# An attention block on one core: GpSimd takes the normalisations, the softmax sums are kept apart, and the last tiles go out singly

## The chip, the cores and the metric

The kernel runs on one core of a Trainium2 chip. A core has five engines with a queue of instructions each: TensorE (PE, matmuls and transposes), VectorE (DVE), ScalarE (ACT, activation functions by table), GpSimd (POOL) and SyncE (SP, here only a queue for transfers). Each works through its queue in order and waits on semaphores for what other engines produce. PE writes its results into PSUM, which this kernel uses as eight banks of 128 x 512 fp32; ACT and DVE read these here, POOL does not. The metric is the device time of one execution in microseconds.

## What is computed

Eight sequences of 512 tokens with 256 channels, all in fp32, run through one transformer block:

```
x = x + attn(layernorm(x))
x = x + ffn(layernorm(x))      # routed: 4 of 16 blocks of hidden units
x = x + gla(layernorm(x))      # gated linear attention over batches, then a SwiGLU
x = x + ffn(layernorm(x))
```

The change lies in the attention and in the very last store. The attention has 16 heads of 16 channels, and only 307 of the 512 queries of a head keep their result:

```
scores   = q @ k.T / 4
sparsity = scores.max(-1) - scores.mean(-1)
top      = top_k(sparsity, 307)
out      = 0 outside top;  softmax(scores[top]) @ v inside
y        = out @ Wo + bo
layernorm(x) = (x - mean(x)) / sqrt(var(x) + 1e-5)
```

## The kernel before

The block holds all tokens in one SBUF tile, `xres` (128 partitions x 8 batches x 4 token tiles x 256 channels). Instructions are written in program order, tile by tile; a planner then sets the order on each engine by simulating the queues with its own estimates of durations, earlier program order first where several instructions could start. So an instruction can be queued well ahead of where the program has it if its inputs are there. To hold an instruction back, the kernel writes one element of its output with a POOL copy from a tile that is made late (`late` in the code); the true write then has to follow that copy.

**The attention's pipeline.** The work is cut into 128 steps, numbered n: batch, head group m (2), parity e (2) and query tile k (4). For each step `max_one` makes four score tiles of 128 x 512 (contraction over 32 rows, one of four row strips each), and DVE reduces each to its maxima (L490). Sixteen steps later (`LAG`) `exp_one` makes the same scores transposed, ACT takes the exponential (L502), and `weigh` multiplies by the values (L507). `take` moves the sum of a head group to SBUF: the weighted values into `outC`, the softmax denominators by a small transfer on ACT's queue into rows of `den`, one row per batch and head. The maxima go through PE (`place_maxima`, L450) into `neg` and into spare rows of q.

**The fronts.** `front(b)` makes q, k and v of one batch: xn (the normalised tokens), its transposes (L357), the copy `xnT` and a copy `xcT` with the mean over tokens taken off, and then the projections q, k (L384) and v (L423) with their evictions (L397, L402, L414, L432). It is a generator, taken in pieces between the groups of scores. In steps 0 to 13 (`LEAD`) there are no exponentials yet, and the pieces of the fronts 0 and 1 are spread over them (`alone` is true); from step 14 on front b+2 runs while batch b has its exponentials.

**The statistics.** `batch_stats` gives mean and variance by `bn_stats` and `bn_aggr` on DVE (L275, L276), the root on ACT (L279), then on DVE the reciprocal (L280) and the shift -mean/root (L283). Batch 0's run at the start, batch 1's in step 1, batch 2's in step 5, batch 3's from step 16, those of 4 to 7 together from step 29. The norms themselves run in `front`: on DVE (L344), for batch 1 on ACT (L340). Loads of x for batch 2 onwards hang on maxima (L217). ACT holds one table of functions at a time; Sqrt and Exp are in different ones, and a change costs an `ACT_TABLE_LOAD`.

**The end of attention.** After the last maxima `top_queries` marks the chosen queries (26 rounds on DVE). `weights_of` makes from `den` the factor of each query and row (reciprocal L137, product L138), for six batches together and later for batches 6 and 7. `weigh_outputs` spreads the rows over channels with a matmul on a strip of 32 rows (L150; two batches share a strip, batch 0 with 1 and so on), and DVE multiplies `outC` by it (L153). `out_unit` projects two batches for one token slice (L163), with the eviction on ACT and the addition on POOL; the other slices are projected later (L849).

**The store.** In the last routed layer each pair of batches of a token slice is added in one DVE instruction (L969) and stored in one transfer (L972).

## Time and profile before

Four runs took 1624.45 to 1631.8 us, median 1628.25. The profile is of one execution.

| | us |
|---|---|
| the profiled execution | 1630.65 |
| its span, first to last instruction | 1628.7 |
| PE busy | 1591.7 (98%) |
| DVE busy | 971.6 (60%) |
| ACT busy | 676.5 (42%) |
| POOL busy | 348.8 (21%) |
| first group of scores starts | 16.1 |
| first exponential starts | 69.9 |
| last `outC` of attention by DVE starts after | 603.84 |
| last addition by DVE starts | 1624.97 |

PE's busy time is modelled and includes waits inside a group of matmuls, so a busy PE need not be PE at its peak; the granted clock is in a row of its own. In a list of groups each line has the source line, engine, operation, output and inputs with shapes, the count, the busy time in us with the mean ns of one, and the idle time ahead of it with the instruction that ended it. In a list by time each line has start, duration, engine, source line and operation; `[1.40 <-ACT e L502]` says that the engine was idle for 1.40 us until that instruction ended.

### The profile page before, as it was taken

What the parts mean: (1) busy time and instruction counts of PE and PEld (TensorE: products, weight loads), DVE (VectorE), ACT (ScalarE), POOL (GpSimd) and SP (SyncE); (2) the same over time, 40 slices, a digit from 0 to 9 for tenths busy, and PEclk for the clock granted to TensorE, in tenths of its full rate; (3) what the DMA queues carried; (4) which work ended last, traced back from release to release, by engine and by line L of the source; (5) the groups of instructions that cost most, each with busy time, mean ns of one, the idle gap of its engine ahead of it and who ended that gap; (6) DMA issues with size and microseconds to landing.
All of it is one profiled execution on the core that took longest, in us unless ns stands there. A gap on an engine that the chain in (4) does not pass through costs nothing.

```text
span 1628.7 us, 19814 instructions
## 1 busy us (share of the span) xinstructions
PE 1591.7 (98%) x7444; PEld 814.3 (50%) x7444; DVE 971.6 (60%) x2007; ACT 676.5 (42%) x1215; POOL 348.8 (21%) x403
## 2 busy tenths in 40 slices
PE   7999999999999999999989999999999999999999
PEld 3323233233233256665564566545655655766666
DVE  6877777676777885447753566367265633344342
ACT  2365666556565844352346124522621452121010
POOL 2111111110010033125432343145234320000000
PEclk8999999999999999999999999999999999999999
DMA  3100000000000033000000001000000010011100
GB/s 107 43 3 3 2 2 3 2 3 3 2 3 3 3 91 105 19 22 13 1 0 1 1 0 27 1 0 1 1 0 1 1 27 0 21 33 39 40 27 26
DMA packets 24951, 27.62 MB, mean 17 GB/s; under 512 B 6872, under 2 KB 21400, under 8 KB 24856
## 3 DMA queue, kind: packets, MB, share of 16 engines
q1 hardware_dynamic: 24040, 25.31, 5.4%
q8 instruction: 58, 0.95, 0.2%
q10 hardware_dynamic: 816, 1.05, 0.2%
q14 instruction: 37, 0.30, 0.1%
HBM read 21.24 MB, written 4.33 MB: 16 GB/s over the span
## 4 chain that ended last, share of the span: by engine, by line
PE 78%; DVE 11%; ACT 4%; POOL 3%; issue 2%; DMA 1%; SPq 0%; ACTq 0%; POOLq 0%; DVEq 0%
PE y_ps L964 16%; PE h_ps L984 11%; PE s L487 9%; PE s L498 8%; PE av L507 8%; PE swi_ps L1011 7%; PE proj_ps L1097 7%; DVE pr L1130 2%; DVE pr L1120 2%; PE q_ps L384 2%; PE k_ps L384 2%; PE gla_y L1222 2%; PE v_ps L423 2%; PE chT_ps L821 2%; POOL o L1147 2%
## 5 line engine op out<-in xcount | busy, mean ns | idle before, releaser
L490 DVE TENSOR_REDUCE mx<-s 128x1 f32<-128x512 f32 x512 | 328.1, 683 | 120.5 <-PE s L498 63.5
L502 ACT ACTIVATE e<-s 128x512 f32<-128x512 f32 x512 | 276.4, 597 | 184.8 <-PE s L498 106.5
L487 PE MATMUL s<-k,q 32*128 32x512 f32 x1024 | 303.5, 649 | 3.0 <-ACT k L414 2.4
L498 PE MATMUL s<-q,k 32*128 32x512 f32 x1024 | 297.3, 642 | 0.1
L984 PE MATMUL h_ps<-xnT,w 128*128 128x512 f32 x512 | 230.1, 598 | 4.1 <-ACT h L992 4.1
L964 PE MATMUL y_ps<-w,h 128*128 128x256 f32 x1024 | 230.8, 381 | 2.7 <-DVE h L993 2.7
L964 PEld LDWEIGHTS y_ps<-w,h 128*128 128x128 f32 x1024 | 192.8, 191 | 39.3 <-issue 10.1
L984 PEld LDWEIGHTS h_ps<-xnT,w 128*128 128x128 f32 x512 | 95.2, 191 | 112.8 <-issue 106.3
L507 PE MATMUL av<-e,va 128*32 128x512 f32 (+1 forms) x1240 | 144.9, 532 | 4.6 <-ACT e L502 3.2
L993 DVE TENSOR_TENSOR h<-h,mk 128x512 f32<-128x512 f32 x128 | 98.5, 783 | 78.9 <-ACT h L992 61.2
L487 PEld LDWEIGHTS s<-k,q 32*128 32x128 f32 x1024 | 94.3, 185 | 96.2 <-DVE mx L490 52.4
L992 ACT ACTIVATE h<-h_ps,b 128x512 f32<-128x512 f32 x96 | 65.4, 685 | 174.9 <-PE h_ps L984 174.9
L969 DVE TENSOR_TENSOR xres<-xres,y_ps 128x512 f32<-128x512 f32 x48 | 32.8, 684 | 160.7 <-PE y_ps L964 123.5
L498 PEld LDWEIGHTS s<-q,k 32*128 32x128 f32 x1024 | 90.8, 183 | 75.6 <-ACT e L502 50.7
L1011 PE MATMUL swi_ps<-zT,w_gate 128*128 128x512 f32 x256 | 122.6, 599 | 4.7 <-DVE h L1020 4.6
L1011 PE MATMUL swi_ps<-zT,w_up 128*128 128x512 f32 x256 | 121.4, 594 | 0.0
L964 PE MATMUL y_ps<-w_down,h 128*128 128x256 f32 x512 | 116.9, 380 | 0.0
L1097 PE MATMUL proj_ps<-q_w,rT 128*128 128x512 f32 x256 | 116.1, 594 | 0.3 <-ACT al L1080 0.3
L964 PEld LDWEIGHTS y_ps<-w_down,h 128*128 128x128 f32 x512 | 95.7, 190 | 19.5 <-issue 8.0
L1017 ACT ACTIVATE h<-swi_ps 128x512 f32<-128x512 f32 x64 | 38.2, 596 | 155.4 <-PE swi_ps L1011 155.3
L1147 POOL TENSOR_TENSOR o<-o,pr 128x512 f32<-128x512 f32 (+2 forms) x56 | 81.1, 1449 | 58.6 <-DVE pr L1130 56.6
L507 PEld LDWEIGHTS av<-e,va 128*32 128x32 f32 x1240 | 25.5, 108 | 123.6 <-issue 103.1
(203 smaller groups left out, 1723.6 us busy)
## 6 DMA issues: line engine op xcount, KB each, us to landing
mk<-md SPq DMA_DIRECT2D x32, 256.0 KB
out<-xres SPq DMA_DIRECT2D x16, 256.0 KB
xres<-in_L_attn_a_x SPq DMA_DIRECT2D x7, 512.0 KB
q<-negT SPq DMA_DIRECT2D x128, 2.0 KB
neg<-negT SPq DMA_DIRECT2D x128, 2.0 KB
w<-in_f_w1T SPq DMA_DIRECT2D x1, 1024.0 KB
w<-in_f_w2T SPq DMA_DIRECT2D x1, 1024.0 KB
w_gate<-in_b_w_gateT SPq DMA_DIRECT2D x1, 1024.0 KB
```

Source lines behind the costliest of these rows:

```text
L487: nc.tensor.matmul(s, qs[e][rows, m, bass.ts(k, P)], ks[e][rows, m, :], start=True, stop=True)
L490: nc.vector.tensor_reduce(mx[:, b, m, e, r : r + 1], s, AX.X, ALU.max)
L498: nc.tensor.matmul(s, ks[e][rows, m, bass.ts(kt, P)], qs[e][rows, m, :], start=True, stop=True)
L502: nc.scalar.activation(ex, s, AF.Exp, scale=1.0 / DH**0.5)
L507: nc.tensor.matmul(av[32 * j : 32 * j + 32, queries], va[:, 8 * kt + 4 * m + j, e, :], es[j][:, queries], start=(kt == 0), stop=(kt == 3 a ...
L964: nc.tensor.matmul(y[0][:, bass.ts(i, D)], h[f][:, bass.ts(2 * u + i, P)], w[:, f, :], start=(f == 0), stop=(f == NF - 1),)
L984: nc.tensor.matmul(ps, w1[:, c, bass.ts(f, P)], xT[g][:, c, :], start=(c == 0), stop=(c == NC2 - 1),)
L992: nc.scalar.activation(hf, ps, AF.Relu, bias=b1[:, f : f + 1])
L993: nc.vector.tensor_tensor(hf, hf, mk[g][:, f, :], ALU.mult)
L1011: nc.tensor.matmul(ps, w[:, c, bass.ts(f, P)], zT[g][:, c, :], start=(c == 0), stop=(c == NC2 - 1),)
L1097: nc.tensor.matmul(ps, rT[b // G4][:, c, bass.ts(b % G4, P)], q_w[:, c, m], start=(c == 0), stop=(c == NC2 - 1),)
L1147: nc.gpsimd.tensor_tensor(dst, dst, src, ALU.add)
```

## The change

- Batches 1 and 2: means and variances come from ACT (`sum_stats`: four Identity and four Square activations with accumulated sums, batch 1's in step 1, batch 2's one per step from step 2). Batches 3 to 7 keep `bn_stats` on DVE, now without pauses, one tile a step from step 16.
- Roots of batches 1 to 7: on POOL, by a first guess from the bits of the number and three Newton rounds (`one_by_root`, 14 small operations), not by ACT's Sqrt. Batch 0 keeps Sqrt, followed by an Exp of one column.
- Norms: `norm` on POOL, four instructions a batch, for all batches but 0; for batches 3 to 7 at i = 12 of the 16 steps before their front, with the bias of Wo right after. The bias row is loaded in step 5 and added to batches 0 to 2 in step 11.
- Evictions in the lead: the values of fronts 0 and 1 are copied by ACT and get their bias on POOL; one more q of front 0 goes to ACT; `xcT` of batch 2 goes to ACT.
- `den` becomes two tiles, one for batches 0 to 5 and one for 6 and 7, both set to 1.0 at the start. A batch's rows move to strip b mod 4, so that the two batches of a pair lie on different strips. `weigh_outputs` does one pair at a time, and the projections of batches 0 and 1 come before the weighing of 4 and 5. The second `weights_of` covers rows 64 to 127.
- `mx` has slots for four batches, used in turn.
- In the last group of the last layer each batch is added and stored by itself.

```diff
-        def weights_of(batches, late, late_form):
-            rows = slice(16 * batches[0], 16 * batches[-1] + 16)
+        def row_of(b, m, e):
+            return 32 * (b % 4) + 16 * (b // 4) + 8 * e + 4 * m
+        def weights_of(rows, i, late, late_form):
...
-            nc.vector.reciprocal(rden[rows, :], den[rows, :])
+            nc.vector.reciprocal(rden[rows, :], den[i][rows, :])
...
-        def weigh_outputs(batches):
-            picks = itertools.cycle((bank, bank_m))
-            for u in range(2):
-                for m in range(NC2):
-                    for b in batches[u::2]:
-                        strip = bass.ts(b // 2, 32)
+        def weigh_outputs(b):
+            for m in range(NC2):
+                for c in (b, b + 1):
+                    strip = bass.ts(c % 4, 32)
...
+            for i in range(2):
+                nc.gpsimd.memset(den[i], 1.0)
...
+            def one_by_root(rs, var, scale):
+                n = rs.shape[1]
+                v = a1.tile([P, n], F32, tag="ln_v", name="ln_v")
+                u = a1.tile([P, n], F32, tag="ln_u", name="ln_u")
+                nc.gpsimd.tensor_scalar(v, var, scale, LN_EPS, ALU.mult, ALU.add)
+                nc.gpsimd.tensor_scalar(
+                    rs.bitcast(I32), v.bitcast(I32), -0.5, float(0x5F3759DF), ALU.mult, ALU.add
+                )
+                for _ in range(3):
+                    nc.gpsimd.tensor_tensor(u, v, rs, ALU.mult)
+                    nc.gpsimd.tensor_tensor(u, u, rs, ALU.mult)
+                    nc.gpsimd.tensor_scalar(u, u, -0.5, 1.5, ALU.mult, ALU.add)
+                    nc.gpsimd.tensor_tensor(rs, rs, u, ALU.mult)
+
+            def sum_stats(b, late):
...
+                own = a2.tile([P, L], F32, tag="e", name="ln_x", bufs=10)[:, 0:D]
+                for i in range(4):
+                    nc.gpsimd.tensor_copy(sums[0:1, i : i + 1], late())
+                    nc.scalar.activation(
+                        own, xres[:, b, i, :], AF.Identity, accum_out=sums[:, i : i + 1]
+                    )
+                    yield
+                nc.gpsimd.tensor_scalar(less, sums, -1.0 / D, None, ALU.mult)
+                for i in range(4):
+                    nc.gpsimd.tensor_copy(squares[0:1, i : i + 1], late())
+                    nc.scalar.activation(
+                        own, xres[:, b, i, :], AF.Square, bias=less[:, i : i + 1],
+                        accum_out=squares[:, i : i + 1],
+                    )
+                    yield
+                one_by_root(rs, squares, 1.0 / D)
...
+                norm(b, ALU.add)
+                yield
+
+            def norm(b, op=ALU.subtract, eng=nc.gpsimd):
+                xn = a2.tile([P, 4, D], F32, tag="xn", name=f"xn{b}", bufs=1)
+                for k in range(4):
+                    mean, rs = ln[b, k]
+                    eng.tensor_scalar(xn[:, k, :], xres[:, b, k, :], mean, rs, op, ALU.mult)
+                normed[b] = xn
...
-                nc.scalar.activation(rs, mv[:, :, 1], AF.Sqrt, bias=eps)
-                nc.vector.reciprocal(rs, rs)
...
-                nc.vector.scalar_tensor_tensor(sh, mv[:, :, 0], -1.0, rs, ALU.mult, ALU.mult)
+                if late is not None:
+                    one_by_root(rs, mv[:, :, 1], 1.0)
+                else:
+                    nc.scalar.activation(rs, mv[:, :, 1], AF.Sqrt, bias=eps)
+                    nc.scalar.activation(root, rs[:, 0:1], AF.Exp)
+                    nc.vector.reciprocal(rs, rs)
...
-                    if alone and b > 0:
+                    if b in (1, 2):
                         nc.scalar.mul(mean, xsum[:, c : c + 1], -1.0 / L)
                         nc.scalar.activation(xcT[:, c, :], ps, AF.Identity, bias=mean)
...
-                        if alone and (b > 0 or e == 0):
+                        if alone and (b + m > 0 or e == 0):
...
+                        if alone:
+                            nc.scalar.copy(home, v)
+                            nc.gpsimd.tensor_tensor(home, home, bias, ALU.add)
+                        else:
+                            nc.vector.tensor_tensor(home, v, bias, ALU.add)
...
-                    for _ in near.get(n, ()):
-                        pass
+                    if n == 1:
+                        for _ in early[1]:
+                            pass
+                    if n > 1:
+                        next(early[2], None)
...
+                    if (n - LEAD) % 16 == 12 and batch + 3 < NB:
+                        norm(batch + 3)
+                        add_bias(batch + 3)
...
-            weigh_outputs(range(NB - 2))
-            last = outC[NB - 3][0:1, 1, 0:1]
-            weights_of(range(NB - 2, NB), last, last)
+            for b in (0, 2):
+                weigh_outputs(b)
             for k in range(2):
-                for b in range(0, NB - 2, 2):
+                out_unit(tail, k, 0)
+            weigh_outputs(4)
+            last = outC[5][0:1, 1, 0:1]
+            weights_of(slice(P // 2, P), 1, last, last)
+            for b in (2, 4):
+                for k in range(2):
                     out_unit(tail, k, b)
-            weigh_outputs(range(NB - 2, NB))
+            weigh_outputs(6)
...
-            if i == 1 and half == 1:
+            if last and k == 3 and b == NB - 2:
+                if half == 1:
+                    x = xres[:, b + i, k, :]
+                    nc.vector.tensor_tensor(x, x, y[0][:, bass.ts(i, D)], ALU.add)
+                    nc.sync.dma_start(out=out_v[:, b + i, k, :], in_=x)
+            elif i == 1 and half == 1:
```

## The prediction

> **What bounds the kernel now.** I read the page's table of forty slices first, then the busy time in chosen stretches, VectorE's groups in one of them, and the instructions in order of time where TensorE is seen to wait.

> ```profile
> PE   7999999999999999999989999999999999999999
> PEclk8999999999999999999999999999999999999999
> ```

> TensorE (PE) is busy nearly throughout; an edit on another engine pays only where PE is held or slowed. That is slice 0, parts of the attention stage (up to 583 us), and the step to the output projection. In the stretches below the columns are length, PE, PE weight loads, VectorE (DVE), ScalarE (ACT), GpSimd (POOL), granted clock, DMA share, GB/s.

> ```profile
> 18.00:20.00 2.00, 2.00 (x5) 0.80 (x6) 1.91 (x5) 1.58 (x4) 0.17 (x1) 0.50 0.19 59
> 26.00:28.00 2.00, 2.00 (x10) 0.51 (x9) 0.00 (x0) 0.00 (x0) 0.00 (x0) 0.53 0.00 0
> 28.00:72.00 44.00, 43.28 (x189) 19.20 (x185) 42.63 (x90) 14.75 (x28) 12.57 (x19) 1.00 0.21 64
> 74.00:76.00 2.00, 2.00 (x6) 0.50 (x9) 0.42 (x1) 0.36 (x1) 0.00 (x0) 0.50 0.00 0
> ```

> From 18 to 28 us PE runs at half clock and DVE waits for it. From 28 to 72 the clock is full and DVE is occupied for 42.6 of 44 us while ACT and POOL are two thirds idle. At 72 the clock halves again, for 7 us. DVE's groups in 28 to 72:

> ```profile
> L490 DVE TENSOR_REDUCE mx<-s 128x1 f32<-128x512 f32 x57 | 35.6, 676 | 3.0 <-PE s L487 2.9
> L432 DVE TENSOR_TENSOR va<-v_ps,bv 128x256 f32<-128x256 f32 x8 | 3.0, 409 | 0.0
> L275 DVE BATCH_NORM_STATS2 ln_st<-xres 128x6 f32<-128x256 f32 x5 | 2.0, 408 | 0.1
> L369 DVE TENSOR_SCALAR xcT<-xnT_ps,xmean 128x512 f32<-128x512 f32 x2 | 1.5, 751 | 0.1
> L344 DVE TENSOR_SCALAR xn<-xres,ln_mv,ln_rs 128x256 f32<-128x256 f32 x4 | 1.4, 395 | 0.0
> ```

> All but the 57 maxima is work that the change takes off DVE, bar one of the five statistics. From 79 us on the chain of waits is PE almost alone, except where a square root comes among ACT's exponentials:

> ```profile
> 112.29 1.28 ACT L279 ACT_TABLE_LOAD   x1
> ...
> 113.90 1.28 ACT L502 ACT_TABLE_LOAD   x1
> 114.13 1.06 DVE L283 SCALAR_TENSOR_TENSOR ln_sh<-ln_mv,ln_rs 128x4 f32<-128x4 f32 x1
> ...
> 115.84 1.04 PE L507 MATMUL av<-e,va 128*32 128x512 f32 x2 [1.40 <-ACT e L502]
> ```

> Two table loads, and PE waits for an exponential. The same is seen at 195.6 and 197.2. At the end of attention:

> ```profile
> 584.94 2.48 DVE L153 TENSOR_TENSOR outC<-outC,nrm_ps 128x512 f32<-128x512 f32 x4 [1.21 <-PE nrm_ps L150]
> ...
> 587.42 4.83 DVE L153 TENSOR_TENSOR outC<-outC,nrm_ps 128x512 f32<-128x512 f32 x8
> ...
> 591.11 9.33 PE L163 MATMUL ao_ps<-wo_a,outC 128*128 128x256 f32 x42 [0.23 <-DVE outC L153]
> ...
> 600.38 3.69 PE L150 MATMUL nrm_ps<-nrm,spread 32*128 32x512 f32 x8
> ```

> Twelve products on DVE, 0.61 us apart, and the projection can go on only after the tenth; later four matmuls on one strip of 32 rows follow one another, 0.92 us each.

> **Part 1, the start (0 to 16.1 us): 0.** Added: the Exp that reads the roots of batch 0 before the reciprocal overwrites them, so the reciprocal waits for a table load (1.283, as the others) and an activation of one column (0.202): +1.48. Removed: batch 1's square root, at 15.08 on ACT, waits for its x, and k's eviction stands behind it until 15.29 though its matmuls ended at 13.71: -1.5. Ends: -1.5 (Exp hidden) and +1.5 (k waits for something else).

> **Part 2, the lead (28 to 72): -5.2.** DVE loses eight value evictions (in pairs of 0.66 in the chain: 2.65), four norms of batch 2 (1.3), its statistics, reciprocal and shift (2.2 with POOL's copy), and two centred copies with their means (1.7): 7.8 in all, leaving 42.6 - 7.8 = 34.8. PE's own work there at full clock: 14 groups of four score matmuls at 1.03 (0.62 and 0.41 in the chain later) 14.5, values 7.6, k 4.3, q 3.4, transposes 2.3, the rest 1: 33. Two engines with 35 and 33 us will wait for each other: DVE idles 1.4 of 44 now, I allow 4, and the stretch takes 38.8. Ends: -7.8 and 0.

> What hides the moved work: ACT is busy 14.75 of these 44 us and gets sixteen sums (0.52 apart by batch 1's norms, plus 0.2 for reading the accumulator: 11.5), eight copies (0.4, below the 0.479 of L1102's 384 columns: 3.2), one q and the centred copies (2.6). POOL is busy 12.6 and gets two root chains of 14 small operations (0.17 to 0.19 each by its one-element copies and the 128x2 product: 2.6), eight norms (0.556 by the 128x256 form at L1229: 4.4), eight additions (0.72 by L1087: 5.8) and sixteen one-element copies (2.8); the three biases are there already. Both end at 31 to 32 of 39. Queued behind ACT's sums, which wait for POOL's copies, are the evictions of q, k and v, and PE's pieces wait for these. Batch 1's norms were ready at 20.5 and used at 37.7; now sums from 18, roots and norms end near 30. SP's queue keeps its loads; the bias row is asked for four steps earlier.

> **Part 3, the half clock: -1.7.** 72 to 79 costs 3.5 against full speed. It follows two steps with hardly any pieces and DVE as the brake. With PE's share up it may not come: even odds, half its price. Ends: -3.5 and 0. The first one (18 to 28, worth 5) follows an idle gap at 13.7 to 16.1 that should shrink to 0.8; I leave it and keep -5 for the range. [...]

> **Part 4, no table switches: -4.8.** At 112 to 117 the groups of scores start 4.86 us apart instead of 2.1, with a transpose of 0.28 among them: 2.5 lost. At 195.62 to 199.68 it is 4.06 instead of 1.8: 2.3. Both go with the Sqrt, the shift and the four norms on DVE. Ends: -3.2 (PE's bare idle, 1.40 and 1.80) and -5.3. The new roots and norms of batches 3 to 7 lie on POOL, which is busy 3 to 7 of each 40 us; xn is made four steps (17 us) ahead of use. Behind them stand the one-element copies that release the statistics on DVE; a root chain or norms with bias (2.6; 2.2 + 2.35) end within about one step of 4.2. I take nothing; ends 0 and +4 (one such wait), and -1.5 for three later bursts of norms off DVE.

> [...]

> **Part 5, weights pair by pair: -4.4.** The products start at 584.9 as before; batches 0 and 1 are done after four (587.4) and PE projects both slices of them, 3.44, to 590.9. Then two strips at a time: 1.72 for batches 4 and 5, to 592.7; projections 6.9, to 599.6. The second weights need the twelfth product (594.5), a reciprocal (3.35) and a product (0.7 to 1.4): 599.7. Batches 6 and 7 take 1.8 on two strips, not 3.69; two projections end at 605.0, against 609.4. What follows there is PE's work (39.7 of 40 us busy). Ends: -5 and -2.5 (only the strips and half the wait). Two memsets (0.45 each, a quarter of L254's) fit POOL's pause at 3.3 to 6.7.

> **Part 6, the last tile: -0.6.** The last addition is 256 wide, 0.41 instead of 0.69; the store is half (128 KB). Now the store takes 3.0 from issue at 1625.7; the first 128 KB load took 3.0 too, so between 0 and -1: -0.3.

> Sum: 0 - 5.2 - 1.7 - 4.8 - 4.4 - 0.6 = -16.7. The profiled execution took 1630.65 (span 1628.7 and 2 around it), so 1614; the median of four is 2.4 lower: **1612**.

> **Rivals.** *Full clock all through* (chance 0.17): both halvings go, 5 + 1.7 more: 1605. For: the gap before the first shrinks. Against: one halving came without a gap.
> *The lead gives nothing* (0.20): ACT's evictions wait behind sums and PE is held where DVE held it; parts 2 and 3 go: 1619. For: PE's 33 us leave little room.
> *It doesn't do what it says* (0.12): the planner orders each queue by its own estimates and puts POOL's norms and bias ahead of the copies that DVE's statistics of batches 3 to 7 need; two or three waits of 4 us, less DVE's slack of 1.2 a step: 1612 + 8 to 12, 1620 to 1624.
> *The other side* (0.06): in steps 2 to 13 of the lead each sum of batch 2 holds ACT, and so PE, by the time of four norms, 2.2 us: 12 x 2.2 = 26, giving 1638. It decides from 1.4 us a step. Against: POOL has 8 us free in 39.

> **Numbers.** My forecast has 0.45. Measurement tells about 0.5% (8 us) from no change, so faster means below 1620. The forecast and full clock are faster but for 0.01, two thirds of "gives nothing" too: 0.75. The third rival, the rest of the second: 0.18. Slower: 0.07. Low end: with the clock full, 1605, and two more from parts 2 and 4: 1603. High end: the third rival's 1624. Outside lie the other side (0.06), some 0.05 below and 0.05 above.

> **What would show it.** One table load before the first exponential and none to 583; first scores still near 16; exponentials from about 65 instead of 69.9; no PE wait of 1.4 near 112 or 195; L163's matmuls from 587.5 and out at 605; a last store of 128 KB. Wrong it would be if ACT's evictions in the lead waited for POOL, or if DVE's statistics after 72 us did.

## The result: 0.17% slower, and the profile after

The changed kernel takes 1630.78 us (median of 52 runs, 1627.72 to 1633.92) against 1627.35 us for the kernel before (79 runs): a ratio of 1.0017, 95% interval 1.0011 to 1.0023. Forecast were 1612 us and a range of 1603 to 1624. The time is outside the range, and "within 0.5%" had a chance of 0.18.

The expected gain of 16.7 us is missing, and 3.4 more. The page of the changed kernel shows hardly a trace of that in its forty slices:

```profile
PE   7889999999999999999989999999999999999999
PEclk9999999999999999999999999999999999999999
```

A slice is 41 us long, and a stop of 7 us is lost in a "9" or an "8". The stretches that the prediction used show it (length, PE, PE weight loads, DVE, ACT, POOL, clock, DMA share, GB/s), in the changed kernel:

```profile
18.00:20.00 2.00, 2.00 (x10) 0.87 (x8) 1.89 (x4) 0.87 (x4) 1.00 (x8) 1.00 0.00 0
26.00:28.00 2.00, 1.93 (x10) 0.93 (x11) 2.00 (x4) 0.00 (x0) 1.38 (x8) 1.00 0.37 97
28.00:72.00 44.00, 35.95 (x163) 15.67 (x163) 30.43 (x54) 18.30 (x46) 25.80 (x54) 0.92 0.19 60
74.00:76.00 2.00, 2.00 (x12) 0.70 (x8) 2.00 (x4) 1.17 (x3) 0.00 (x0) 1.00 0.00 0
```

Both of the old half-clock spells are gone. But in 28 to 72 us PE is busy for 36 of 44 us where it was 43.3, DVE for 30.4 where it was 42.6, and the clock is 0.92: somebody holds both. POOL, 12.6 before, has 25.8. PE's three longest waits between 14 and 130 us (waiting line, releaser, us in all, times, longest):

```profile
PE s L538 <- DVE mx L541: 7.0, 1, 7.0
PE q_ps L431 <- ACT xnT L407: 5.3, 1, 5.3
PE s L538 <- ACT k L461: 2.8, 2, 2.0
```

The names ACT and DVE mislead here. What held these two engines is read from the instructions in order of time. The first stop (start, duration, instruction, and in brackets the engine's idle time before it and what ended it):

```profile
39.97 2.34 POOL L387 TENSOR_TENSOR xres<-xres,bo 128x1024 f32<-128x1024 f32 x1 [0.90 <-DMA bo<-in_L_attn_a_bo]
...
43.62 2.34 POOL L387 TENSOR_TENSOR xres<-xres,bo 128x1024 f32<-128x1024 f32 x1
45.90 0.29 POOL L301 COPY ln_sm<-mx 1x1 f32<-1x1 f32 x2
46.11 0.51 ACT L302 ACTIVATE ln_x<-xres,ln_sm 128x256 f32<-128x256 f32 x1 [6.33 <-POOL ln_sm L301]
...
46.62 0.58 ACT L407 ACTIVATE xnT<-xnT_ps 128x512 f32<-128x512 f32 x1
...
47.34 2.07 PE L431 MATMUL q_ps<-xnT,wq 128*128 128x512 f32 x2 [5.30 <-ACT xnT L407]
```

Two additions of the output bias, wanted by nobody for another 500 us, stand in POOL's queue ahead of a copy of one element. That copy lets ACT take batch 2's next sum of squares; behind the sum, in ACT's queue, waits an eviction, and PE waits for the eviction. The second stop:

```profile
86.48 0.19 POOL L276 TENSOR_SCALAR ln_v<-ln_mv 128x4 f32<-128x4 f32 x1 [0.77 <-DVE ln_mv L334]
...
90.11 0.20 POOL L284 TENSOR_TENSOR ln_rs<-ln_rs,ln_u 128x4 f32<-128x4 f32 x1
90.42 4.85 POOL L317 TENSOR_SCALAR xn<-xres,ln_mv,ln_rs 128x256 f32<-128x256 f32 x4
...
95.36 2.34 POOL L387 TENSOR_TENSOR xres<-xres,bo 128x1024 f32<-128x1024 f32 x1
97.64 0.17 POOL L332 COPY ln_st<-mx 1x1 f32<-1x1 f32 x1
...
97.84 0.43 DVE L333 BATCH_NORM_STATS2 ln_st<-xres 128x6 f32<-128x256 f32 x1 [8.15 <-POOL ln_st L332]
...
99.12 1.22 PE L538 MATMUL s<-k,q 32*128 32x512 f32 x1 [7.01 <-DVE mx L541]
```

Batch 3's roots, norm and bias, written for step 26, run at step 19, before the copy that DVE's statistics of batch 4 wait for; the maxima stand behind the statistics on DVE. For 4 us PE does nothing at all. The clock is halved around each stop, for 6.8 us from 45.0 and again from 96.2; here are the rows of the second:

```profile
94.00:98.00 4.00, 0.00 (x0) 0.00 (x0) 0.15 (x1) 0.00 (x0) 3.92 (x5) 0.77 0.01 2
98.00:102.00 4.00, 2.88 (x9) 1.02 (x10) 2.92 (x6) 0.73 (x2) 0.58 (x2) 0.50 0.01 4
```

So both things came that the prediction named as signs of being wrong: evictions of ACT in the lead waited for POOL (behind a sum that did), and so did DVE's statistics after 72 us. Of the other readings that it asked for, some hold: between 5.7 and 583 us there is no table load, the first scores start at 16.9, and the projection's first matmul starts at 587.76 (in the kernel before six started at 589.32 and the rest from 591.11). Two don't: the first exponential starts at 73.2 instead of 65, and the projection of this stage is out at 607.1 instead of 605.

**Balance by stretch.** The table gives, for the main stretches between two instructions that all kernels have, the length in the kernel before and the difference to it (us, from the start times in the trace of one profiled execution each). The kernels right of the changed one are the experiments below; "both" and the unchanged kernel were profiled twice.

| stretch (in maxima of the attention) | before, us | before again | changed | bias late | norms held | both | both again | weights alone | last version |
|---|---|---|---|---|---|---|---|---|---|
| 1st to 9th (old half clock) | 10.79 | 0.00 | -3.96 | -3.95 | -3.95 | -3.95 | -3.95 | -3.70 | -3.95 |
| 9th to 64th (the lead) | 41.89 | +0.01 | +6.76 | +1.12 | +8.88 | -0.48 | +0.66 | +0.13 | -1.74 |
| 64th to 73rd (half clock at 72) | 13.41 | 0.00 | -3.44 | -3.44 | -3.44 | -3.44 | -3.44 | 0.00 | -3.44 |
| 73rd to 97th | 25.92 | +0.01 | +8.13 | +5.45 | -0.19 | -0.20 | -0.19 | +0.08 | -0.20 |
| 97th to 113th (first table switch) | 19.55 | 0.00 | -2.71 | -2.71 | +1.38 | -2.79 | -2.78 | 0.00 | -2.79 |
| 161st to 193rd (second) | 36.06 | 0.00 | -2.91 | -2.91 | -2.91 | -2.91 | -2.91 | 0.00 | -2.91 |
| 193rd to 512th | 318.80 | 0.00 | -1.25 | -1.27 | -1.26 | -1.27 | -1.27 | 0.00 | -1.30 |
| weights to first hidden unit | 42.85 | 0.00 | -3.16 | -3.11 | -3.16 | -1.48 | -3.16 | -3.17 | -3.16 |
| from there through the next two layers | 771.31 | +3.14 | +2.61 | +2.71 | +2.87 | +1.37 | -1.77 | +2.44 | +0.71 |
| last layer, to its last matmul | 226.54 | 0.00 | +0.85 | +0.85 | +0.85 | +0.85 | +0.85 | 0.00 | 0.00 |

The unchanged kernel's second profile is the yardstick: the attention repeats to 0.02 us, while the long stretch after it differs by 3.14 us between two executions of the same program. Differences there say nothing about an edit. Nor does one of less than some 2 us in the lead, where "both" differs by 1.14 between its two profiles: a half-clock spell follows PE's wait of 2.0 us near 32 in some executions (bias late, norms held, both again) and not in others (changed, both).

### The profile page after: what moved, and what is told of

Same layout as the page of the kernel before. It is cut to its first block, busy times and chain, and to the rows that moved or that the text cites. A ratio compares the mean times of both kernels' runs of the same rounds, so it can differ in the third digit from the quotient of the medians.

```text
span 1629.2 us, 19915 instructions
## 1 busy us (share of the span) xinstructions
PE 1580.0 (97%) x7444; PEld 810.5 (50%) x7444; DVE 955.0 (59%) x1946; ACT 681.2 (42%) x1249; POOL 396.2 (24%) x506
## 4 chain that ended last, share of the span: by engine, by line
PE 78%; DVE 10%; ACT 4%; POOL 4%; issue 2%; DMA 1%; SPq 0%; POOLq 0%; ACTq 0%; DVEq 0%
PE y_ps L1016 16%; PE h_ps L1042 11%; PE s L538 9%; PE s L549 9%; PE av L558 8%; PE swi_ps L1069 7%; PE proj_ps L1155 7%; DVE pr L1188 2%; DVE pr L1178 2%; PE q_ps L431 2%; PE k_ps L431 2%; PE v_ps L470 2%; PE gla_y L1280 2%; PE chT_ps L873 2%; POOL o L1205 2%
## 5 line engine op out<-in xcount | busy, mean ns | idle before, releaser
L538 PE MATMUL s<-k,q 32*128 32x512 f32 x1024 | 296.4, 645 | 9.9 <-DVE mx L541 7.0
L549 PE MATMUL s<-q,k 32*128 32x512 f32 x1024 | 293.4, 641 | 0.3 <-DVE mx L541 0.3
L924 POOL TENSOR_TENSOR xres<-xres,b 128x512 f32<-128x512 f32 x32 | 40.1, 1271 | 207.6 <-ACT row L863 185.2
```

What stands on the lines that cost most here:

```text
L538: nc.tensor.matmul(s, qs[e][rows, m, bass.ts(k, P)], ks[e][rows, m, :], start=True, stop=True)
L549: nc.tensor.matmul(s, ks[e][rows, m, bass.ts(kt, P)], qs[e][rows, m, :], start=True, stop=True)
```

## The experiments

**Theory**: POOL's single queue ate the gain, by what the planner put ahead of one-element copies. **Rivals**: the work moved to ACT is too much by itself; half-clock spells come anyway; what is gained is taken back later. Ratios are to the kernel before on the same chip.

| kernel | us, median | ratio, 95% interval |
|---|---|---|
| bias late | 1621.16 | 0.9962 (0.9949 to 0.9976) |
| norms held | 1626.34 | 0.9995 (0.9986 to 1.0005) |
| both, and added means | 1614.58; again 1613.55 | 0.9923 (0.9910 to 0.9935); 0.9920 (0.9907 to 0.9933) |
| added means alone | 1628.38 | 0.9994 (0.9982 to 1.0006) |
| both, values on DVE | 1614.18 | 0.9907 (0.9892 to 0.9922) |
| both, old weights | 1617.30; again 1619.00 | 0.9930 (0.9917 to 0.9944); 0.9943 (0.9930 to 0.9955) |
| before, with the weights alone | 1625.22; again 1623.58 | 0.9989 (0.9978 to 0.9999); 0.9977 (0.9965 to 0.9988) |
| before, unchanged, again | 1628.78 | 1.0009 (0.9997 to 1.0020) |
| last version | 1610.37 | 0.9896 (0.9878 to 0.9913) |

**1. The biases late.**

```diff
-                    if n == 5:
-                        nc.gpsimd.tensor_copy(bo[0:1, 0:1], maximum_of(n))
-                        nc.sync.dma_start(out=bo, in_=t["L0_attn_a_bo"].partition_broadcast(P))
-                    if n == 11:
-                        for b in range(3):
-                            add_bias(b)
...
                         norm(batch + 3)
-                        add_bias(batch + 3)
+                    if n == 91:
+                        nc.gpsimd.tensor_copy(bo[0:1, 0:1], maximum_of(n))
+                        nc.sync.dma_start(out=bo, in_=t["L0_attn_a_bo"].partition_broadcast(P))
+                    if 92 <= n <= 120 and n % 4 == 0:
+                        add_bias((n - 92) // 4)
```

> The changed kernel with the row of output biases loaded at step 91 and all eight additions of it to the residual made after that, instead of at steps 5, 11, 12 and on; everything else as changed. Theory (POOL's one queue: what stands ahead of a one-element copy sets when ACT's sums and DVE's statistics may run): the two 2.34 us additions no longer stand ahead of batch 2's squares, the 5.3 us wait of PE at 47 and the half clock behind it go, and nothing takes their place; the maxima from step 32 on come about 6 us earlier than in the changed kernel, the second stall at 99 stays at 5 to 7 us (only its one addition of 2.34 us is gone), and the time is 1622 to 1625, some 0.3 to 0.5% below the changed kernel's. Rival (the moved sums and evictions load ACT too much by themselves): the same squares are late because of ACT, PE waits 3 us or more near 47 all the same, and the time stays within 2 us of the changed kernel's 1630.8.

PE's three longest waits in 14 to 130 us:

```profile
PE s L538 <- DVE mx L541: 4.6, 1, 4.6
PE s L538 <- ACT k L461: 2.8, 2, 2.0
PE q_ps L431 <- ACT xcT L413: 0.7, 1, 0.7
```

The 5.3 us wait is gone, though ACT has exactly the sums and evictions it had; the rival that these are too much falls. The other stop lost 2.4 us, the length of the one addition that stood in it. The lead is 5.6 us shorter than in the changed kernel, and the time 9 us (by the ratios), to just below what was expected. In the profiles 1.7 us of that lie at the start, where no part of this edit acts.

**2. The later norms held to their step.**

```diff
-            def norm(b, op=ALU.subtract, eng=nc.gpsimd):
+            def norm(b, op=ALU.subtract, eng=nc.gpsimd, late=None):
                 xn = a2.tile([P, 4, D], F32, tag="xn", name=f"xn{b}", bufs=1)
+                if late is not None:
+                    nc.gpsimd.tensor_copy(xn[0:1, :, 0:1], late.unsqueeze(1).to_broadcast([1, 4, 1]))
...
-                        norm(batch + 3)
+                        norm(batch + 3, late=maximum_of(n - 1))
```

> The changed kernel with each later norm (batches 3 to 7) begun by a one-element copy of the maximum of the step where it is asked for, so that it can't be put ahead of the copies for the statistics of batches 4 to 7; the additions of the biases follow it as before. Theory: the 4.85 us of batch 3's norm and the 2.34 us of its bias leave the place ahead of the copies at 90 to 97.6, the 7.0 us wait of PE at 99 falls to under 2.5 us (Newton's 3.9 us stay ahead), the half clock after it goes, and the time is 1622 to 1626; the first stall at 47 stays at 5.3 us. Rival (ACT and DVE are too full there in any case): the wait moves some steps on, where the norm now stands, and sums to 5 us or more again; the time stays within 2 us of the changed kernel's.

The same here:

```profile
PE q_ps L433 <- ACT xnT L409: 5.3, 1, 5.3
PE s L540 <- ACT k L463: 2.8, 2, 2.0
PE s L540 <- DVE mx L543: 2.8, 1, 2.8
```

The first stop is as it was, the second is gone from its place (73rd to 97th: 8.32 us less than in the changed kernel), and a wait of 2.8 comes some steps later, where the norm (4.85) and bias (2.34) now stand ahead of the next copies: +1.38 instead of -2.71 in the following stretch. So theory and rival are each half right: the order put the stop there, but 7.2 us of POOL's work in one piece are too long anywhere among those copies. The time fell by 3.6 us by the ratios, to the upper end of what was expected; in the profile the lead is 2.1 us longer than in the changed kernel, with a half-clock spell at 33.4.

**3. Which form of the norm is slow.** In the changed kernel the norms of batches 1 and 2 take 0.55 us each on POOL, those of 3 to 7 take 1.22. They differ in the operation (adding a negated mean, subtracting a mean) and in where the mean lies. Here batches 3 to 6 add, and batch 7 has all four forms.

```diff
+                    less = a1.tile([P, n], F32, tag=f"ln_less{key}", name="ln_less")
+                    nc.gpsimd.tensor_scalar(less, mv[:, :, 0], -1.0, None, ALU.mult)
...
+                    for k, mean, op in (
+                        (0, mv[:, 12, 0:1], ALU.subtract), (1, less[:, 13:14], ALU.subtract),
+                        (2, mv[:, 14, 0:1], ALU.add), (3, less[:, 15:16], ALU.add),
+                    ):
+                        nc.gpsimd.tensor_scalar(
+                            xn[:, k, :], xres[:, b, k, :], mean, rs[k], op, ALU.mult
+                        )
...
-                        norm(batch + 3)
+                        norm(batch + 3, ALU.add)
```

> The changed kernel with the norms of batches 3 to 6 made by adding a negated mean; the four norms of batch 7 are made in four ways, in this order: subtracting a mean that lies every second element (as changed), subtracting a mean that lies in a row of its own, adding a negated mean that lies every second element, adding one from a row of its own. Theory A (the subtraction is what takes 1.22 us instead of 0.55): the four take 1.22, 1.22, 0.55, 0.55. Rival B (where the mean lies): 1.22, 0.55, 1.22, 0.55. Rival C (the two engines at once on their memory, that is, what DVE does beside it): no pattern by form, and the added norms of batches 3 to 6 also take about 1.2. With A or B the norm of batch 3 takes 2.2 instead of 4.85, so copy and statistics come some 2.6 us earlier at 97, the second stall of PE falls from 7.0 to about 4.4 us, and the time is 1626 to 1629; with C it is the changed kernel's.

The four instructions in order of time:

```profile
348.84 1.23 POOL L325 TENSOR_SCALAR xn<-xres,ln_mv,ln_rs 128x256 f32<-128x256 f32 x1 [10.35 <-PE xnT_ps L425]
350.06 1.21 POOL L325 TENSOR_SCALAR xn<-xres,ln_less,ln_rs 128x256 f32<-128x256 f32 x1
351.26 0.55 POOL L325 TENSOR_SCALAR xn<-xres,ln_mv,ln_rs 128x256 f32<-128x256 f32 x1
351.80 0.55 POOL L325 TENSOR_SCALAR xn<-xres,ln_less,ln_rs 128x256 f32<-128x256 f32 x1
```

Theory A: the subtraction takes 2.2 times as long as the addition here, wherever the mean lies. Rival C falls too, since it is the operation that sorts them at all other places: the sixteen added norms of batches 3 to 6 took 0.55 to 0.56 us, and the twenty subtracted ones of the changed kernel 1.22 to 1.24. The second stop fell from 7.0 to 4.6 us, as expected.

**4. All three together.** The edits of 1 and 2, and the added mean for batches 3 to 7.

> The changed kernel with both edits (biases from step 91 on, later norms held to their step) and with the later norms made by adding a negated mean instead of subtracting the mean. Theory: neither stall of PE is there, the gains of the weights, of the removed table switches and of the first half clock are all that is left, and the time is 1615 to 1620, 0.5 to 0.75% below the kernel before. Rival (the half clock comes wherever PE has once waited, or the lead's other 1.95 us wait at 32 grows): a half-clock spell stands somewhere else in the first 130 us and the time is 1622 to 1626. Rival (the removal of stalls is worth nothing since later stages take it back): 1628 or more.

In 14 to 130 us PE waits for this alone:

```profile
PE s L546 <- ACT k L469: 2.8, 2, 2.0
PE q_ps L439 <- ACT xcT L421: 0.7, 1, 0.7
PE s L557 <- DVE mx L549: 0.3, 1, 0.3
```

1614.58 us, and 1613.55 when run again:

> The kernel with both edits again, beside the one with the old weights. If the gain of the weights stays: 2.5 to 3.5 us below that; if the clock takes it back: less than 1.5 us below it. 1613 to 1616.

This is 0.95% below the changed kernel (by the ratios, 15 to 16 us), and just below what the theory expected: two orders in one queue and one slow form cost these 15 to 16 us. The stretches agree: 7.2 us in the lead and 8.3 between the 73rd and 97th maxima. A spell of half clock from 34.15 us stands in one of its two profiles and not in the other (+0.66 against -0.48 in the lead), after the same wait of 2.0 us.

**5. Was DVE the brake in the lead?**

```diff
-                        if alone:
-                            nc.scalar.copy(home, v)
-                            nc.gpsimd.tensor_tensor(home, home, bias, ALU.add)
-                        else:
-                            nc.vector.tensor_tensor(home, v, bias, ALU.add)
+                        nc.vector.tensor_tensor(home, v, bias, ALU.add)
```

> The kernel with both edits (biases late, later norms held and by addition), with all evictions of values back on DVE with their bias, as in the kernel before. Theory (in the lead PE's own work is the bound, so what DVE lost there bought little): DVE takes 3 us more between 24 and 66 us, and the time is within 1.5 us of that kernel's 1614.6. Rival (the prediction's: DVE is the brake there and gains what it loses): 2.5 to 4 us longer, 1617 to 1618.5, with PE waiting for maxima between 36 and 66 us.

24 to 66 us, first in "both", then in this kernel:

```profile
24.00:66.00 42.00, 38.97 (x186) 16.99 (x179) 34.93 (x62) 21.40 (x54) 21.34 (x63) 1.00 0.20 64
```

```profile
24.00:66.00 42.00, 39.52 (x177) 17.68 (x177) 36.56 (x69) 17.72 (x43) 15.02 (x51) 0.96 0.21 64
```

DVE gets its eight evictions back (3.0 us), and nothing is lost: 1614.18 us, and of PE's waits for maxima between 36 and 66 us only the one of 0.3 is there that "both" has too. The lead is +0.81 with a half-clock spell at 32 to 36 as in the second profile of "both" (+0.66). The chain of the last version, which has no stop in the lead, says why (start, us, what):

```profile
48.50 1.07 PE s L546 x8
49.57 1.06 PE k_ps L439 x2
50.62 1.43 PE s L546 x8
52.05 1.92 PE v_ps L478 x8
53.98 1.07 PE s L546 x8
55.05 1.92 PE v_ps L478 x8
```

PE goes from piece to piece without a pause for 21 us. It is the bound there, beside a DVE that is nearly as full. The run shows it for these 3.0 us; the other 4.8 that the change takes off DVE by the prediction's count were not put back.

**6. What the weights are worth.** Alone, on the kernel before (with the smaller tiles for maxima, marks and statistics that make room for it); and the other way, the old weights in "both". The main part of the edit:

```diff
-            weigh_outputs(range(NB - 2))
-            last = outC[NB - 3][0:1, 1, 0:1]
-            weights_of(range(NB - 2, NB), last, last)
+            for b in (0, 2):
+                weigh_outputs(b)
             for k in range(2):
-                for b in range(0, NB - 2, 2):
+                out_unit(tail, k, 0)
+            weigh_outputs(4)
+            last = outC[5][0:1, 1, 0:1]
+            weights_of(slice(P // 2, P), 1, last, last)
```

> The kernel before with only the last part of the change but one: the sums of the exponentials in two tiles, rows by pairs, the outputs weighed pair by pair between the units of the output product (and the smaller tiles for maxima, statistics and marks that make room for it). Theory: the 3.2 us that the changed kernel gains at this place reach the end, and the time is 3 to 4 us below the kernel before (1623.5 to 1624.5). Rival (what is gained there is lost again to PE's clock in the feed-forward part, as the spell of half clock that moved from 600 to 640 in the kernel before to 720 to 760 in the changed one suggests): within 1 us of the kernel before.

> The kernel with both edits, with the weights of the outputs as in the kernel before (one tile of sums, six batches at once, then two). Theory (most of what is gained there is lost again to a half clock near 745 to 760 us, which the kernel before doesn't have): 0.5 to 1.5 us longer than that kernel's 1614.6, with the step to the projection 2.5 to 3.5 us longer and the half clock near 745 gone. Rival (the gain is real and stays, the clock's spells fall where they like): 2.5 to 3.5 us longer, 1617 to 1618.

Then all four beside each other:

> The kernel before with only the weights of the outputs by pairs, now beside its pair. If the gain stays: 2.5 to 3.5 us below the kernel before. If the clock takes it back: within 1.5 us of it, with a half clock near 750 us that the unchanged kernel beside it doesn't have.

> The kernel with both edits and the old weights, beside its pair. 1614.5 to 1619; the profile shows whether the half clock at 740 to 750 is there again or whether a spell comes and goes from one execution to the next.

> The kernel before, unchanged, for a second profile beside its pair. If its half clock from 17 to 28 us belongs to the kernel, it is there again and the first maxima of the second group come as late (the ninth about 3.7 us later than in the kernel with both edits); if it hangs on when the first rows arrive, it is gone as in the kernel with the weights alone and the profiled span is about 4 us shorter, at 1624 to 1626. Its time is within 0.2% of the kernel before either way.

At its place the edit gives 3.17 us, in every kernel that has it (but for a half-clock spell at 587.6 us in one profile of "both"). My theory was that the clock takes it back at 740 to 760 us, where the changed kernel and the weights alone have a spell and the kernel before had none. The second profile of the unchanged kernel refutes it. Here is PE at that place in the first profile and then in the second:

```profile
755.16 0.70 PE L964 MATMUL y_ps<-w,h 128*128 128x256 f32 x2 [1.95 <-DVE h L993]
756.36 8.90 PE L964 MATMUL y_ps<-w,h 128*128 128x256 f32 x40 [0.49 <-DVE h L993]
```

```profile
756.51 0.70 PE L964 MATMUL y_ps<-w,h 128*128 128x256 f32 x2 [1.95 <-DVE h L993]
757.70 7.57 PE L964 MATMUL y_ps<-w,h 128*128 128x256 f32 x26 [0.50 <-DVE h L993]
```

The same two waits, and then 40 matmuls in 8.9 us or 26 in 7.6: in the second the clock is halved for 3.41 us from 758.52. It is the execution and not the edit. Over that whole stretch the kernels with the edits lie between -1.77 and +2.87 us, the two profiles of the kernel before at 0 and +3.14. Old weights cost "both" 3.7 us by the ratios of the last comparison, and as much against the kernel of experiment 5 in the one before it; each ratio is known to some 2 us. So the gain stays, and fits its 3.2. On the kernel before it measured only 1.8 and 3.8 us (ratios 0.9989 and 0.9977), although that kernel also lost the half clock at 17 to 28 us, worth 3.7 in the profiles. That these two don't add up to 7 in the times has a reason on record: the profiled execution of the kernel before is not a usual one. Its spells make 30.7 us at half clock, a granted clock of 0.991 (0.990 in the second profile). The 57 other executions of it that were run beside the experiments have 0.990 to 0.997, on average 0.9935, which is some 21 us. Six of them, at 0.996 and 0.997, can't have had both the spell at 17 and the one at 72 us, since these two alone make 0.9948. So the early spells are not in every execution, and what their removal is worth on average is less than the profiles say; how much less stays open.

**7. A version with three more edits.** On top of "both":

```diff
-                    if n > 1:
+                    if n > 3:
                         next(early[2], None)
...
-                    nc.scalar.activation(root, rs[:, 0:1], AF.Exp)
                     nc.vector.reciprocal(rs, rs)
+                    nc.scalar.activation(root, rs[:, 0:1], AF.Exp)
...
-            if last and k == 3 and b == NB - 2:
-                if half == 1:
-                    x = xres[:, b + i, k, :]
-                    nc.vector.tensor_tensor(x, x, y[0][:, bass.ts(i, D)], ALU.add)
-                    nc.sync.dma_start(out=out_v[:, b + i, k, :], in_=x)
-            elif i == 1 and half == 1:
+            if i == 1 and half == 1:
```

> The kernel with both edits and three more: the sums of batch 2 start two steps later (step 4 instead of 2), so that no copy for them stands behind batch 1's norm on POOL while k's eviction waits behind the sum on ACT; the Exp that loads its table stands behind the reciprocal of the first roots instead of ahead of it; the last tile's two halves are added and stored together, as in the kernel before. Theory: the 2.0 us wait of PE at 32 goes, the first scores come 0.7 us earlier, the last PE wait of 0.6 us goes while the last store is 0.5 longer: 1611 to 1613. Rival (the wait comes back where batch 2's norm is now late, at step 14, near 66 us): 1614 to 1617.

```profile
PE s L546 <- ACT k L469: 0.9, 1, 0.9
PE s L546 <- ACT va L496: 0.7, 1, 0.7
PE s L557 <- DVE mx L549: 0.3, 1, 0.3
PE q_ps L439 <- ACT xcT L421: 0.2, 1, 0.2
```

1610.37 us, 1.04% below the kernel before, and below what was expected. The 2.0 us wait at 32 us is gone and did not come back (the lead -1.74), and the last layer lost its +0.85. The gain over "both" is read from these stretches; in the times the intervals of the ratios still overlap.

## Why the prediction was wrong, step by step

- **Part 4, new work on POOL at no cost ("I take nothing; ends 0 and +4 (one such wait)"), is the step that failed.** It cost 8.3 us against the repaired kernel. The mechanism was on the list, as the third rival with a chance of 0.12, but priced at 4 us a wait less DVE's slack. Four terms were too small: the later norms subtract, 1.22 us each where I took 0.556 from a row that multiplies and adds (+2.65); Newton's fourteen operations were 0.19 to 0.20 long but started 0.28 apart, 3.9 us and not 2.6; roots, norm and bias came together, not "a root chain or norms with bias"; and half clock stood around each of the two stops (6.8 us from 45.0 and from 96.2).
- **Part 2, -5.2 with 0 as its worse end, failed in two ways.** The lead got 6.8 us longer. The same queue cost 7.2 us there: "the three biases are there already" counted POOL's busy time, not its order, and the planner put two additions ahead of batch 2's copies. That the bias row was asked for four steps earlier made this possible, but was not tested by itself. The rival on the other side (sums of batch 2 hold ACT, and so PE, in every step) had the right chain of waits; but one stop came, not twelve, and POOL's order made it. And without that stop the lead gives 0.5 us or loses 0.7, not -5.2. PE's own work there at full clock, put at 33, was mis-sized: the last version's lead is 40.15 us, with at most 2.1 of waits, so PE's work there is some 38. The score groups take 1.07 and 1.43 in turn, where I took 1.03 from a stretch with fewer pieces. The rival "The lead gives nothing" was right about the size of the lead in the repaired kernel, but its way there (ACT's evictions behind sums) holds for one wait of 2.0 us alone.
- **Part 3, -1.7**: measured -3.44; the spell at 72 us is gone in every kernel with the moved norms, as the rival "Full clock all through" had it. Why is not shown. The first spell, kept for the range at -5, went too: -3.96, and -3.70 with the weights alone. In all of these PE's wait before the first scores is 0.9 us, where it was 2.4 and 2.7. The two are argued to be connected, not shown.
- **Part 4, the table switches, -4.8**: measured -2.71 and -2.91, together -5.6, a little beyond the end of -5.3; the three bursts, taken at 0 with an end of -1.5, gave -1.25. The mechanism was right.
- **Part 5, -4.4**: measured -3.16, inside its ends. The twelfth product ended at 596.1 instead of 594.5, behind statistics of the next layer on DVE, and the last two strips were done at 603.5 instead of 601.5.
- **Part 6, -0.6**: measured +0.2. What follows the last matmul is 0.6 shorter, but PE now waits 0.59 us for the first half's addition, which reads the PSUM tile that the second half's matmuls write, and the last layer is 0.85 longer. This wait was not in the sum.
- **Part 1, 0**: +0.81 in the changed kernel, within its ends; in the last version, with the Exp behind the reciprocal, -1.21, but the start moves by 1.7 us between kernels that are equal there.
- **The base.** The sum started from one execution, of 1630.65 us. That I took 2.4 off for the median was right in size; that the spells which I then removed might be among those 2.4 was not thought of. By the granted clocks (experiment 6) they are in part: the profiled execution has 30.7 us at half clock and the average one some 21.

The kernel that does what the change says took 1614.58 and 1613.55, near the forecast of 1612, but that is luck: the lead is not in it, and the two half-clock spells are.

## What to carry to other kernels

Ask of an engine that gets new work not only whether it has time, but what stands in its queue behind the new work and who waits for that. POOL was 24% busy, and two pieces of 6 and 11 us cost 15 us because one-element copies that release other engines stood behind them. Work wanted late should be made unable to start early, in pieces shorter than the waiters' slack.

Before an engine is named the brake of a stretch, the other full engine's work is to be summed at the durations of that stretch itself.

## What the runs showed of the hardware

```profile
31.20:34.61 3.41, 2.28 (x12) 1.14 (x16) 1.78 (x4) 2.12 (x6) 2.47 (x6) 1.00 0.48 154
34.61:38.02 3.41, 3.41 (x24) 1.64 (x24) 2.58 (x5) 1.84 (x7) 2.20 (x6) 1.00 0.03 7
```

```profile
30.74:34.15 3.41, 1.95 (x8) 0.98 (x8) 1.71 (x5) 2.45 (x7) 2.47 (x6) 1.00 0.41 143
34.15:37.56 3.41, 3.41 (x13) 1.45 (x12) 1.53 (x3) 0.51 (x2) 1.13 (x6) 0.50 0.06 18
```

Nine of the 58 spells, near 72 us and at the step to the projection, follow less than 1 us of idle time and stay unexplained.
